# Moving four steps of a hand-ordered attention: modulation, its weights' loads, x2's product, a transposition of maxima

## The chip, the cores and the metric

The kernel runs on one core of a Trainium2 chip. The metric is device time in microseconds (us) of one launch. The kernel before takes 2960.37 us, the median of three runs (2959.13 to 2960.70). One more run was profiled; every duration below comes from it.

## The reference, cut to what matters

A batch of 8 sequences (256 channels x 512 steps) goes through four residual layers. The change touches the first two only.

```
x  = x + L0(x, cond, Wq, Wo)          # masked attention, 8 heads, q = k = v, over 512 positions
x  = x + L1(x, cond, W_emb, ...)      # below, 16 heads, over 256 positions
x  = x + L2(...)                      # oscillator, 512 steps in sequence
x  = x + L3(...)                      # GRU, 512 steps in sequence

# L1
scale, shift = split(cond @ W_emb + b_emb)
xn  = rms_norm(x, g_norm) * (1 + scale) + shift          # the modulation
q, k, v = heads(xn @ W_qkv);  q, k = rms_norm(q, g_q), rms_norm(k, g_k)
o   = softmax(q k' / sqrt(32)) v
out = o + o @ W_out                                      # added to x: "x2"
```

## The kernel before, in words

There are two parts, one after the other: `attention` (L0 and L1) and `scans` (L2 and L3). The change lies in `attention`; `scans` needs all of x2.

`attention` is a list of slots, g = -5 to 79. In each slot a fixed order of calls, written out by hand at the end of the function, gives each engine its instructions; every engine runs its own in that order. The work of the 8 sequences overlaps: `at(g, rel, n)` gives the sequence b and the step r of it that falls in slot g, 8 slots (U) to a sequence.

L0, for each sequence b and each half e of the heads, has four chunks of keys:
- `project` (slots 8b-5 and 8b-4; TensorE line 176, VectorE line 179, ScalarE line 182) makes q; `project_out` transposes it a slot later.
- `scores0` (TensorE line 198, four products of 512 columns a slot; ScalarE line 203 copies them to SBUF).
- `maxima0` (VectorE line 208) takes each row's maximum over a chunk, one chunk a slot.
- `rows0` runs after the fourth chunk, in each slot g = 3 mod 4 from -1 to 59: four 128x128 transpositions (TensorE line 216, one for each chunk's maxima), a copy (ScalarE line 218), then on SyncE's queue a write of the row to DRAM (`row`, line 221) and its load back to all partitions (`bc`, line 222, 1 MB). `bc` has one buffer.
- `weights0` (VectorE line 226 subtracts `bc`, ScalarE line 227 takes the exponential), `values0` (TensorE line 238), `weigh0` (VectorE lines 255 and 256), `masked_out` (line 265).

L1, for each sequence, runs some 11 slots later:
- `normalize` and `modulate` (lines 277 to 296) use `shift` and `G`, made once by `modulation`.
- `modulation` (lines 123 to 148) has two small transpositions, 32 fp32 products of `wemb` with the 8 conditions (line 135; each product is two instructions on TensorE, so the trace counts 64), seven short VectorE steps that end in `shift`, and the addition of the identity to `wout_sb` (line 148). It is called in slot 4.
- `qkv` (TensorE line 305, ScalarE lines 318 and 320), `qkv_norm` (VectorE line 326, GpSimd lines 328 to 330), and a slot later `qkv_out` (TensorE line 340, ScalarE line 344) make v, k and q, one sixth a slot; for the last two sequences two sixths a slot.
- `maxima1` (TensorE line 352, VectorE line 360), `rows1` (line 365), `weights1` (TensorE lines 375 and 384, ScalarE line 390) and `values1` (TensorE line 154, VectorE lines 164 and 165) run for four chunks c of heads, in slots HEADS to HEADS+5. HEADS is 19, 27, 35, 43, 51, 59, 65 and 71.
- `modulated_out` makes x2 (TensorE line 405, VectorE line 410) in two halves, in slots OUT: (25, 27), (33, 35), (41, 43), (49, 51), (57, 59), (65, 67), (71, 72), (77, 78). `modulated_turn` transposes it one slot later.

All of these but `values0` take their PSUM results from one pool of six banks (`bank`), handed out in the order of the calls; a new product waits until the one that had the bank six calls ago has been read.

The weights `wqkv_sb` (3 MB, first read in slot 13) and `wout_sb` (1 MB, first read by line 148, then in slot 25) are loaded on SyncE's queue before the first slot, after `wemb`, the second sequence's x and `wo_sb`. Every DMA of the kernel is issued there.

Of the kernel before, what the change touches and what calls it, by code (L numbers as in the profile page):

```python
# [8 lines left out]
F32 = mybir.dt.float32  # L9
# [5 lines left out]
P = 128  # L15
B, T, D = 8, 256, 512
NJ = D // P
# [7 lines left out]
def attention(ctx, tc, cst, x, cond, wqT, woT, w_emb, b_emb, g_norm, w_qkv, g_q, g_k, w_out, follow):  # L25
# [21 lines left out]
    U = 8  # L47
# [31 lines left out]
    with tc.manual_schedule():  # L79
        nc.sync.dma_start(wq_sb, wqT.rearrange("(k p) e -> p k e", p=P))  # L80
        load(0)
        cst["rest"]()
        vec = wp.tile([12, P], F32, name="vec")
        nc.sync.dma_start(vec[0:8, :], b_emb.rearrange("(f p) -> f p", p=P))
        nc.sync.dma_start(vec[8:12, :], g_norm.rearrange("(f p) -> f p", p=P))
        gq_sb = wp.tile([P, 1], F32, name="gq_sb")
        gk_sb = wp.tile([P, 1], F32, name="gk_sb")
        for i in range(4):
            nc.sync.dma_start(gq_sb[32 * i : 32 * i + 32, :], g_q.unsqueeze(1))
            nc.sync.dma_start(gk_sb[32 * i : 32 * i + 32, :], g_k.unsqueeze(1))  # L90

        wemb = [
            two.tile([P, 2 * D], F32, tag=tag, name=f"wemb_{k}", bufs=bufs)
            for k, (tag, bufs) in enumerate((("qT", 1), ("kT", 1), ("vt", 2), ("vt", 2)))
        ]
        for k in range(NJ):
            nc.sync.dma_start(wemb[k], w_emb[k * P : (k + 1) * P, :])
        load(1)
        wo_sb = fone.tile([P, 2, 256], F32, name="wo_sb")
        nc.sync.dma_start(wo_sb, woT.rearrange("(k p) e -> p k e", p=P))  # L100
        wqkv_sb = wp.tile([P, NJ, 3 * D], F32, name="wqkv_sb")
        nc.sync.dma_start(wqkv_sb, w_qkv.rearrange("(k p) f -> p k f", p=P))
        wout_sb = wp.tile([P, NJ, D], F32, name="wout_sb")
        nc.sync.dma_start(wout_sb, w_out.rearrange("(k p) f -> p k f", p=P))

    gqs = wp.tile([P, 1], F32, name="gqs")
    mhalf = wp.tile([P, 16], F32, name="mhalf")
# [15 lines left out]
    def modulation():  # L123

        nc.vector.tensor_scalar_mul(gqs, gq_sb, SC)
        pv = bank([P, 28], "pvs")
        nc.tensor.transpose(pv, cst["vecs"], ident[0:28, 0:28])
        nc.vector.tensor_copy(cst["vecS"], pv)
        pv = bank([P, 12], "pv")
        nc.tensor.transpose(pv, vec, ident[0:12, 0:12])  # L130
        nc.vector.tensor_copy(vecT, pv)
        pe = bank([P, 8, B], "pe")
        for f in range(8):
            for k in range(NJ):
                nc.tensor.matmul(
                    pe[:, f, :],
                    lhsT=wemb[k][:, f * P : (f + 1) * P],
                    rhs=condT[:, k, :],
                    start=(k == 0),
                    stop=(k == NJ - 1),  # L140
                )
        nc.vector.tensor_tensor(ssT, pe, vecT[:, 0:8].unsqueeze(2).to_broadcast([P, 8, B]), ALU.add)
        nc.vector.tensor_scalar_add(G, ssT[:, 0:NJ, :], 1.0)
        nc.vector.tensor_tensor(G, G, vecT[:, 8:12].unsqueeze(2).to_broadcast([P, NJ, B]), ALU.mult)
        nc.vector.tensor_copy(shift, ssT[:, NJ:8, :])

        for c in range(NJ):
            nc.vector.tensor_add(wout_sb[:, c, c * P : (c + 1) * P], wout_sb[:, c, c * P : (c + 1) * P], ident)
# [57 lines left out]
    def maxima0(b, e, qc):  # L206

        nc.vector.tensor_reduce(  # L208
            mxp0[e].rearrange("p q (h i) -> p q h i", i=32)[:, qc, :, 0], scs[b, e, qc], AX.X, ALU.max
        )  # L210

    def rows0(b, e):

        pt = bank([P, NJ, P], f"pm0_{b}_{e}")
        for qc in range(NJ):
            nc.tensor.transpose(pt[:, qc, :], mxp0[e][:, qc, :], ident)
        mrow = ftwo.tile([P, D], F32, tag="mrow", name=f"mrow0_{b}_{e}", bufs=1)
        nc.scalar.copy(mrow, pt.rearrange("p q n -> p (q n)"))
        bc = bcs[b, e] = ftwo.tile([P, 4, D], F32, tag="bc", name=f"bc_{b}_{e}", bufs=1)
        row = dram.tile([4, D], F32, tag="row", name=f"row_{b}_{e}", bufs=2)  # L220
        nc.sync.dma_start(row, mrow.rearrange("(h i) n -> h i n", i=32)[:, 0, :])
        nc.sync.dma_start(bc, row.rearrange("h n -> (h n)").partition_broadcast(P).rearrange("p (h n) -> p h n", h=4))
# [114 lines left out]
    def qkv_out(b, part, m, qr):  # L337
        pt = bank([P, NJ, P], f"ptqk_{b}_{m}_{part}")
        for c in range(NJ):
            nc.tensor.transpose(pt[:, c, :], qr[:, c * P : (c + 1) * P], ident)  # L340
        ts, tag, g = ((qTs, "qT", gqs), (kTs, "kT", gk_sb))[part]
        if m == 0:
            ts[b] = two.tile([P, NJ, 256], F32, tag=tag, name=f"{tag}_{b}", bufs=1)
        nc.scalar.activation(ts[b][:, :, m * P : (m + 1) * P], pt, AF.Copy, scale=g)
# [56 lines left out]
    def modulated_out(b, m):  # L401
        n = f"{b}_{m}"
        ps = bank([P, D], f"psx2_{n}")
        for c in range(NJ):
            nc.tensor.matmul(  # L405
                ps, lhsT=oTs[b][:, c, m * P : (m + 1) * P], rhs=wout_sb[:, c, :], start=(c == 0), stop=(c == NJ - 1)
            )
        x2 = line(f"x2_{n}")

        nc.vector.tensor_tensor(  # L410
            x2.rearrange("p (m j i) -> p j m i", j=NJ, m=NJ),
            ps.rearrange("p (j m i) -> p j m i", j=NJ, m=NJ),
            xs[b][:, m, :].rearrange("p (j m i) -> p j m i", j=NJ, m=NJ),
            ALU.add,
        )
        return x2
# [41 lines left out]
    def leave(kind):  # L458
        for key in [k for k in left if k[0] == kind]:
            yield *key[1:], left.pop(key)  # L460

    with tc.manual_schedule():
        for g in range(-5, OUT[-1][1] + 2):

            if a := at(g, -4, U):
                scores0(a[0], a[1] // 4, a[1] % 4)
            if a := at(g, 2, U):
                values0(a[0], a[1] // 4, a[1] % 4)
            for a in leave("qt"):
                project_out(*a)  # L470
            if g == OUT[-1][1] + 1:
                cst["soon"]()
            for a in leave("x2"):
                modulated_turn(*a)
            if g - 1 in norms:
                modulate(norms.index(g - 1))
            if a := at(g, 1, U):
                weights0(a[0], a[1] // 4, a[1] % 4)
            if (a := at(g, 2, U)) and a[1] % 4 == 3:
                weigh0(a[0], a[1] // 4)  # L480

            if a := at(g, -5, 2):
                left["qt", a[0], a[1]] = project(*a)
            if a := at(g, U + 2):
                masked_out(a[0])
            if g == 4:
                modulation()
            if g in norms:
                normalize(norms.index(g))
            made = [(part, qkv(*part)) for part in parts.get(g, ())]  # L490
            for a in leave("qkv"):
                qkv_out(*a)
            for b in range(B):
                if g in OUT[b]:
                    m = OUT[b].index(g)
                    left["x2", b, m] = modulated_out(b, m)

            for part, lines in made:
                if lines:
                    qkv_norm(*part, *lines)  # L500
                    left["qkv", *part] = lines[1]
            if a := heads(g, 1):
                rows1(*a)
            a, a1 = at(g, -4, U), heads(g, 0)
            last = a and a[1] % 4 == 3
            if last:
                maxima0(a[0], a[1] // 4, 3)
            if a1:
                maxima1(*a1)
            if a2 := heads(g, 2):  # L510
                values1(*a2)
            if a2 := heads(g, 1):
                weights1(*a2)
            if a and not last:
                maxima0(a[0], a[1] // 4, a[1] % 4)
            if last:
                rows0(a[0], a[1] // 4)
            if (a2 := at(g, -7)) and a2[0] > 1:
                load(a2[0])
            if g == U * B + 2:  # L520
                first.close()
                follow()
                for (b, m), d in x2d.items():
                    nc.sync.dma_start(
                        cst["x2T"][:, :, b, m * P : (m + 1) * P], d.rearrange("p (j n) -> p j n", j=NJ)
                    )
# [486 lines left out]
```

## Time and profile before

| | us |
|---|---|
| median of three runs (lowest, highest) | 2960.37 (2959.13, 2960.70) |
| the profiled run: its own time | 2958.41 |
| the profiled run: span, first to last instruction | 2956.6 |
| attention, up to the scan's first product | 881.3 |
| TensorE busy, whole span | 2720.4 |
| VectorE busy | 2124.6 |
| ScalarE busy | 1720.9 |
| GpSimd busy | 1049.1 |

The profile gives, for each engine, busy time by line and by stretch of time, the waits with what released them, and the instructions in order of time. In an "in order of time" view a row is the start, the time from the first start to the last end of a run of equal instructions, the engine, line and operation, out<-in, shape and count; in brackets stands the idle time before it and the engine or DMA that ended it. PE is TensorE, DVE VectorE, ACT ScalarE, POOL GpSimd, SP SyncE. PEclk is the clock granted to TensorE, 1.00 being full speed.

### The profile page before, as it was taken

How to read it: one execution, taken by the hardware profiler on the slowest of the kernel's cores; microseconds unless marked ns; L12 is line 12 of the kernel's file. 1: busy time of each engine (PE TensorE's matmuls, PEld its weight loads, DVE VectorE, ACT ScalarE, POOL GpSimd, SP SyncE). 2: the span in 40 equal slices, each digit the busy share in tenths (PEclk: the TensorE clock that was granted, in tenths of full speed). 3: DMA queues.
4: the chain of work that ended last, by engine and by line, in shares of the span. 5: the costliest groups of instructions: out<-in, count | busy, mean ns of one | idle time of the engine just before them, and what ended most of it. 6: DMA issues, size and time to landing. Idle time of an engine off the chain costs nothing.

```text
span 2956.6 us, 159809 instructions
## 1 busy us (share of the span) xinstructions
PE 2720.4 (92%) x67258; PEld 1930.5 (65%) x67258; DVE 2124.6 (72%) x8948; ACT 1720.9 (58%) x8427; POOL 1049.1 (35%) x2945
## 2 busy tenths in 40 slices
PE   6789999999988999999999999999999999999997
PEld 3234444444546777777777777777777777777776
DVE  4866676666446777777777777777777777777773
ACT  4655566554335666666666666666666666666551
POOL 0233123312313444444444444444444444444442
PEclk7989999999999999999999999999999999999998
DMA  3110101000600000000000000000000000000000
GB/s 143 40 40 29 40 26 47 29 33 23 129 15 4 7 6 7 6 7 7 7 6 7 6 7 7 6 6 7 7 7 7 6 7 7 6 7 6 6 7 6
DMA packets 27559, 57.60 MB, mean 19 GB/s; under 512 B 2816, under 2 KB 17164, under 8 KB 24788
## 3 DMA queue, kind: packets, MB, share of 16 engines
q1 hardware_dynamic: 26836, 47.36, 5.3%
q8 instruction: 526, 8.62, 1.2%
q14 instruction: 197, 1.61, 0.2%
HBM read 40.15 MB, written 7.21 MB: 16 GB/s over the span
## 4 chain that ended last, share of the span: by engine, by line
PE 39%; DVE 24%; ACT 5%; issue 3%; ACTq 0%; POOL 0%; DVEq 0%; POOLq 0%
PE pg L744 19%; PE ic L709 18%; DVE icT L901 5%; DVE qn L902 5%; ACT tT L609 4%; DVE hqs L862 3%; DVE own L759 3%; DVE sqmm L858 2%; DVE v L761 2%; DVE hz L789 2%; DVE own L778 1%; ACT sqmm L847 1%; DVE own L784 1%; PE psx L405 1%; ACTq L609 0%
## 5 line engine op out<-in xcount | busy, mean ns | idle before, releaser
L709 PE MATMUL ic<-cT_sb,tT 128*8 128x128 f32 x32736 | 1086.1, 273 | 82.3 <-ACT tT L609 45.6
L709 PEld LDWEIGHTS ic<-cT_sb,tT 128*8 128x8 f32 x32736 | 760.1, 89 | 339.8 <-ACT tT L609 268.5
L744 PE MATMUL pg<-whh_sb,hz 128*32 128x128 f32 x24576 | 820.9, 275 | 49.4 <-DVE hz L789 17.6
L609 ACT ACTIVATE tT<-qn 128x16 f32<-128x16 f32 x2046 | 440.8, 216 | 636.9 <-DVE qn L902 516.4
L744 PEld LDWEIGHTS pg<-whh_sb,hz 128*32 128x32 f32 x24576 | 669.5, 110 | 123.1 <-DVE hz L789 122.9
L901 DVE STREAM_TRANSPOSE icT<-ic 128x64 f32<-128x64 f32 x2048 | 504.2, 246 | 67.6 <-PE ic L709 63.2
L902 DVE SCALAR_TENSOR_TENSOR qn<-icT,hqs 128x16 f32<-128x16 f32 x2048 | 350.7, 171 | 70.1
L704 POOL TENSOR_TENSOR W<-W,cx 128x128 f32<-128x128 f32 x765 | 297.3, 389 | 256.6 <-ACT cx L690 256.4
L697 POOL TENSOR_TENSOR W<-cx,us 128x128 f32<-128x128 f32 x255 | 116.9, 458 | 445.0 <-ACT cx L690 445.0
L858 DVE SCALAR_TENSOR_TENSOR sqmm<-sqmm,qn 128x32 f32<-128x32 f32 x768 | 153.5, 200 | 151.4 <-ACT sqmm L847 122.4
L862 DVE TENSOR_TENSOR hqs<-W,sqmm 128x32 f32<-128x32 f32 x1020 | 199.9, 196 | 46.1 <-DVE own L784 1.0
L723 PE MATMUL gi<-wih_sb,x3T 128*32 128x384 f32 (+2 forms) x3072 | 201.5, 379 | 0.5 <-POOL x3T L914 0.5
L690 ACT ACTIVATE cx<-qn 128x32 f32<-128x32 f32 x1280 | 200.9, 213 | 0.0
L227 ACT ACTIVATE sc<-sc,negT 128x2048 f32<-128x2048 f32 x64 | 128.6, 2010 | 89.2 <-DVE sc L226 79.2
L305 PE MATMUL psqkv<-wqkv_sb,xnT 128*128 128x512 f32 x384 | 174.8, 600 | 0.2 <-DVE oT L165 0.2
L690 ACT ACTIVATE cx<-p 128x32 f32<-128x32 f32 x1020 | 149.8, 217 | 32.4 <-DVE p L857 1.6
L226 DVE TENSOR_TENSOR sc<-sc,bc 128x2048 f32<-128x2048 f32 x64 | 147.8, 2310 | 11.9 <-DMA bc<-row 11.9
L203 ACT COPY sc<-s 128x512 f32<-128x512 f32 x256 | 132.1, 617 | 40.6 <-PE s L198 40.4
L759 DVE STREAM_TRANSPOSE own<-pg 128x128 f32<-128x128 f32 x256 | 84.8, 331 | 94.8 <-PE pg L744 94.8
L208 DVE TENSOR_REDUCE mxp<-sc 128x4 f32<-128x2048 f32 x64 | 145.8, 2279 | 6.7 <-ACT sc L203 6.7
L690 ACT ACTIVATE cx<-q 128x32 f32<-128x32 f32 x1020 | 145.5, 213 | 0.0
L847 ACT ACTIVATE sqmm<-qn 128x32 f32<-128x32 f32 x768 | 140.5, 183 | 0.6
(149 smaller groups left out, 3364.0 us busy)
## 6 DMA issues: line engine op xcount, KB each, us to landing
bc<-row SPq DMA_DIRECT2D x16, 1024.0 KB
x<-in_x SPq DMA_DIRECT2D x8, 512.0 KB
out<-o SPq DMA_DIRECT2D x256, 16.0 KB
wqkv_sb<-in_L_cond_W_qkv SPq DMA_DIRECT2D x1, 3072.0 KB
wih_sb<-in_L_cond_W_ih SPq DMA_DIRECT2D x4, 768.0 KB
whh_sb<-in_L_cond_W_hh SPq DMA_DIRECT2D x4, 768.0 KB
x2d<-x2o SPq DMA_DIRECT2D x11, 256.0 KB
x2T<-x2d SPq DMA_DIRECT2D x11, 256.0 KB
```

What stands on the lines that cost most here:

```text
L305: nc.tensor.matmul(ps, lhsT=xnTs[b][:, c, m * P : (m + 1) * P], rhs=wqkv_sb[:, c, part * D : (part + 1) * D], start=(c == 0), stop=(c == N ...
L609: nc.scalar.activation(tT, src[:, half * HM : (half + 1) * HM, :], AF.Tanh)
L690: nc.scalar.activation(c[:, i], x, AF.Copy, scale=f)
L704: nc.gpsimd.tensor_tensor(W[:, i + 1 : 5], W[:, i + 1 : 5], c, ALU.add)
L709: nc.tensor.matmul(ps[32 * j : 32 * j + B, :], lhsT=tT[k // HM][:, k % HM, :], rhs=cT_sb[:, k, j * P : (j + 1) * P], start=(k == 0), stop= ...
L723: nc.tensor.matmul(gi_ps[rows(j), g0:g1, :], lhsT=x3T[c][:, k, :], rhs=wih_sb[:, k, g0:g1, j * P : (j + 1) * P], start=(k == 0), stop=(k = ...
L744: nc.tensor.matmul(pg_ps[rows(j), :], lhsT=hzs[tau % 3][:, k, 32 * g : 32 * g + 32], rhs=whh_sb[:, k, g, j * P : (j + 1) * P], start=((k, ...
L759: nc.vector.transpose(pgt.rearrange("p m n -> p (m n)"), pg_ps)
L858: stt(mm, sq, LIN[s], qs, ALU.subtract, ALU.mult)
L862: nc.vector.tensor_sub(hq, W[:, s], mm)
L901: nc.vector.transpose(icT.rearrange("p m n -> p (m n)"), ic[:, half * 64 : half * 64 + 64])
L902: stt(qn[:, m2, :], icT[:, :, 0:B], IC[s], hq[:, m2, :], ALU.mult, ALU.add)
```

## The change

- `modulation` is called in slot 1, not 4; its last step, the identity added to `wout_sb` (four VectorE instructions), becomes `add_identity` and is called in slot 8, just ahead of `normalize`.
- The loads of `wqkv_sb` and `wout_sb` become `load_weights`, called at the end of slot -1, behind that slot's `rows0`.
- In each slot, `modulated_out` stands ahead of `qkv_out`. Both run in slots 25, 27, 33, 35, 41, 43, 49, 51, 57, 59, 65 and 71. Only TensorE's order changes by it: `qkv_out` has no VectorE step, and `modulated_out` no ScalarE step.
- `rows0` follows the fourth `maxima0` at once, ahead of `maxima1`, `values1` and `weights1` of the slot. These run beside it in slots 19, 27, 35, 43, 51, 59 (`maxima1`) and 23, 31, 39, 47, 55 (`values1`, `weights1`); in the other slots of `rows0` nothing stands between.

No instruction is added or removed. The diff:

```diff
@@ -98,10 +98,14 @@
-        wqkv_sb = wp.tile([P, NJ, 3 * D], F32, name="wqkv_sb")
+    wqkv_sb = wp.tile([P, NJ, 3 * D], F32, name="wqkv_sb")
+    wout_sb = wp.tile([P, NJ, D], F32, name="wout_sb")
+
+    def load_weights():
+
         nc.sync.dma_start(wqkv_sb, w_qkv.rearrange("(k p) f -> p k f", p=P))
-        wout_sb = wp.tile([P, NJ, D], F32, name="wout_sb")
         nc.sync.dma_start(wout_sb, w_out.rearrange("(k p) f -> p k f", p=P))
@@ -143,6 +147,8 @@
         nc.vector.tensor_copy(shift, ssT[:, NJ:8, :])
+
+    def add_identity():
 
         for c in range(NJ):
             nc.vector.tensor_add(wout_sb[:, c, c * P : (c + 1) * P], wout_sb[:, c, c * P : (c + 1) * P], ident)
@@ -483,17 +489,19 @@
-            if g == 4:
+            if g == 1:
                 modulation()
+            if g == U:
+                add_identity()
             if g in norms:
                 normalize(norms.index(g))
             made = [(part, qkv(*part)) for part in parts.get(g, ())]
-            for a in leave("qkv"):
-                qkv_out(*a)
             for b in range(B):
                 if g in OUT[b]:
                     m = OUT[b].index(g)
                     left["x2", b, m] = modulated_out(b, m)
+            for a in leave("qkv"):
+                qkv_out(*a)
@@ -505,6 +513,7 @@
             if last:
                 maxima0(a[0], a[1] // 4, 3)
+                rows0(a[0], a[1] // 4)
             if a1:
                 maxima1(*a1)
             if a2 := heads(g, 2):
@@ -513,10 +522,10 @@
             if a and not last:
                 maxima0(a[0], a[1] // 4, a[1] % 4)
-            if last:
-                rows0(a[0], a[1] // 4)
             if (a2 := at(g, -7)) and a2[0] > 1:
                 load(a2[0])
+            if g == -1:
+                load_weights()
```

## The prediction, as put on record

> **What bounds the kernel now.** First the busy times by stretch: the first 148 us, the rest of attention, the scans. Columns: us of PE, PEld, DVE, ACT, POOL, then the granted clock, DMA share, GB/s.
>
> ```profile
> 0.00:148.00 148.00, 104.51 (x550) 44.19 (x554) 97.37 (x74) 81.85 (x127) 18.40 (x23) 0.84 0.25 91
> 148.00:881.00 733.00, 680.79 (x4716) 318.87 (x4708) 458.87 (x425) 382.28 (x629) 193.60 (x159) 0.95 0.15 42
> 881.00:2956.60 2075.60, 1935.06 (x62000) 1567.41 (x62000) 1568.38 (x8451) 1256.81 (x7673) 837.13 (x2763) 1.00 0.03 7
> ```
>
> The scans (2075.6 us) hold no changed line and wait for the last x2, so they start earlier or later by what attention gains. From 148 to 881 TensorE is busy 93%: there a wait on TensorE is lost unless a later wait shrinks by it. The first 148 us have 43 us of idle TensorE and no engine that is full; waits decide. So I read the start in order of time, TensorE first:
>
> ```profile
> 23.91 7.27 PE L198 MATMUL s<-qm 32*128 32x512 f32 x24
> 42.16 1.94 PE L238 MATMUL pc<-sc,qtok 128*32 128x512 f32 x8 [10.98 <-ACT sc L227]
> ...
> 59.37 10.60 PE L135 MATMUL pe<-condT,wemb 128*128 128x8 f32 x64
> ```
>
> TensorE stands idle for 10.98 us, then spends 10.60 us in modulation. VectorE beside it:
>
> ```profile
> 39.93 2.28 DVE L208 TENSOR_REDUCE mxp<-sc 128x4 f32<-128x2048 f32 x1
> ...
> 70.00 0.22 DVE L142 TENSOR_TENSOR ssT<-pe,vecT 128x64 f32<-128x64 f32 x1 [9.83 <-PE pe L135]
> ...
> 71.48 2.28 DVE L208 TENSOR_REDUCE mxp<-sc 128x4 f32<-128x2048 f32 x1
> ```
>
> Modulation halts VectorE for 9.83 us; from 71.48 on VectorE runs without a gap to 93.8, so it sets the pace there. The 10.98 us come from the first `bc`: its row is issued at 24.63 (behind 4 MB of weights), `bc` only at 32.99, 7.7 us of it a wait for the row; VectorE's subtraction starts at 37.72.
>
> Then the slots where `rows0` meets L1's work. Slot 31, TensorE, then VectorE:
>
> ```profile
> 348.23 0.38 PE L365 MATMUL pm<-ident,mxp 128*128 128x128 f32 x2
> 348.54 1.07 PE L154 MATMUL pc<-ex,vt 128*32 128x256 f32 x16
> ...
> 352.35 0.66 PE L216 MATMUL pm<-ident,mxp 128*128 128x128 f32 x4
> 354.21 1.14 PE L198 MATMUL s<-qm 32*128 32x512 f32 x8 [1.21 <-DVE oT L165]
> ```
>
> ```profile
> 349.66 2.28 DVE L208 TENSOR_REDUCE mxp<-sc 128x4 f32<-128x2048 f32 x1
> ...
> 353.64 0.42 DVE L165 TENSOR_TENSOR oT<-pc,r 128x256 f32<-128x256 f32 x1
> ```
>
> The maxima that line 216 needs are done at 351.9; `values1` and `weights1` fill TensorE until 352.35, so line 216 waits for nothing. Last, slot 59, where q's transposition does wait:
>
> ```profile
> 687.62 1.11 PE L340 MATMUL ptqk<-ident,qr 128*128 128x128 f32 x4 [3.40 <-POOL qr L330]
> 688.53 4.82 PE L405 MATMUL psx<-wout_sb,oT 128*128 128x512 f32 x8
> ...
> 696.64 1.07 PE L238 MATMUL pc<-sc,qtok 128*32 128x512 f32 x8
> ```
>
> x2's product, whose inputs are ready, queues behind that wait. After 148 us the waits of line 340 on GpSimd sum to 15.6 us (8 of them).
>
> [...] at 156.21 line 216 waits 3.27 us with the next slot's ready scores behind it. [...] the stretch 424 to 429 has a mean clock of 0.66 and 452 to 456, right after slot 39's wait, one of 0.57, each the mean of 3.4 us at 0.50 and the rest at 1.00. [...] the 8 KB row took 7.7 us behind the weights, 1.8 us (54.63 to 56.39) with an empty queue.
>
> **The change, part by part.**
>
> *Modulation and weights (slots -1 to 8).* The loads now stand behind `bc`: row at 24.63, landed 26.4, `bc` issued then, and 4.7 us (32.99 to 37.7) later, at 31.1, it is there instead of at 37.7. The weights follow, 4 MB at some 400 GB/s (the rate at 25 to 30 us), done near 40; first read in slots 8 (93.8 us) and 13 (135.57), so 50 us of cover. `wemb` lies in the first 4 MB of the queue, landed near 21 (rates summed from the stretches of 5 us).
> TensorE: scores of slots 0 and 1 are two thirds of the 7.27 us, to 28.8. Then modulation. Its products run at half clock there (0.50 from 22 to 46 us): from 65 to 70 us, at 0.50, 28 took 5.0 us, 0.179 each, so 64 take 11.4, to 40.6 with the two transpositions. VectorE's steps to `shift` (70.00 to 70.84) end at 41.5, and slot 1's maxima start there, not at 39.93: 1.6 us late. Slot 2's scores come at 40.6 to 43.0, `values0` 0.9 later than 42.16; with half clock lasting a little longer I carry 2.6 us late to slot 4. There the queue finds no modulation: its maxima begin after line 179 at 59.25 + 2.6 + 0.7 = 62.5 instead of 71.48. Gain 8.9. `bc`'s 6.6 us are not added: modulation's own end (40.6) would hide a `bc` of 37.7. Bounds: 6 (half clock goes on to slot 5) and 10.6 (nothing late). The identity's 0.89 us goes to slot 8, where VectorE idles 1.42 (scores' copies) and 1.92 (`bc`) around it: nothing; 0.9 if that cover went.
>
> *x2 first, slots 25 to 57 with half 0.* The transposition did not wait there; order alone. kT's copy comes 3.5 us later and is read two slots on. Nothing; bounds 0 and +0.5 each (ScalarE behind it).
>
> *x2 first and `rows0` early, slots 27, 35, 43, 51.* By slot 27: x2's product starts at 290.45 instead of 292.43, ends 294.0; the transposition (qr ready at 291.9) ends 294.5. x2's addition (0.7) and the maxima (2.28) on VectorE end at 297.0, not 299.0. Line 216 ends 297.4. `maxima1`'s second half still waits for qT, whose copy ScalarE runs at 297.17 to 297.84 behind `normalize`, which is not changed: ends 298.6. Before, line 216 came after that, and the next scores ended at 301.33, held by banks that VectorE frees (2.06 us instead of 1.14). Now VectorE frees them 0.8 earlier and one bank belongs to the already copied maxima: end near 299.8. Gain 1.5 each, 6.0. Bounds 0.7 (bank waits stay) and 2.7 (both waits, 1.49 and 1.21).
> *Slot 19*, no x2: line 216 (1.05) falls into the 4.65 us wait for qT. With the bank, 1.6.
> *Slot 59:* x2's product from 684.2, maxima done 690.8 (from 687.8 + 0.7 + 2.3), `maxima1` ends behind qT's copy (692.9) at 693.6; `values0` there instead of 696.64. Gain 3.0.
> *Slot 65:* the wait of 1.73 goes, but qT's copy, hidden by x2's product until now, shows some 0.6. Gain 1.2. *Slot 71:* the 3.44 goes, 0.8 of copy shows, and a little queueing: 3.1 (bounds 1.5 and 4.8, the latter with x2's product at full clock: 3.6 for 5.29).
>
> *`rows0` early, slots 23, 31, 39, 47, 55.* By slot 31: line 216 now stands behind `rows1` (348.5) and its fourth transposition needs the maxima of 351.9: done 352.25, after about 3.0 us idle. Behind it in TensorE's queue stand `values1` (1.9, to 354.15) and `weights1` (1.95, to 356.1). The next scores wait for banks: the second for `values1`'s result, 1.75 + 0.42 on VectorE after 354.15, so 356.4; the third and fourth for the first exponentials of line 390 (356.8, 357.3). They end at 357.6, before at 355.28: 2.35 lost, five times 11.8. `bc` gains nothing: its one buffer is freed by the next slot's subtraction as before. Bounds: 0.5 each if the maxima come early enough, 5.8 if two half-clock windows follow each wait (each 3.4 us long, 1.7 lost).
>
> *Clock.* One more half-clock window in slot 31's kind, where four of five had one already (+1.7), against the one in slot 71 that should go (-1.7): 0; bounds -5 and +9.
>
> *Sum:* 8.9 + 6.0 + 1.6 + 3.0 + 1.2 + 3.1 = 23.8 gained, 11.8 lost: 12.0 less. The profiled run took 2958.4 (span 2956.6 and 1.8 around it), so 2946.4; the median of the runs is 2.0 above that run: 2948.4.
>
> **Rivals.**
> 1. *The moved transposition makes it slower.* Line 216's wait in slots 23 to 55 sends TensorE to half clock through `values1`, `weights1` and the next slot. For: the wait is near 3 us[...]; after the 3.27 us wait at 156.21 the clock was halved. Against: after 2.80 us at 121.88 it was not. Three windows each: 2.35 + 3 x 1.7 = 7.45, times 5 = 37.3; 13.5 more than the 23.8 gained, so 2973.9. It decides from 23.8 / 5 = 4.8 us a slot.
> 2. *The wait of slots 23 to 55 costs next to nothing*, since the 1.21 us bank wait goes and others shrink: 0.4 each. 2960.4 - 21.8 = 2938.6. For: that wait does end later than the stall; against: VectorE's queue has the maxima behind line 326 in both.
> 3. *The start gains little:* TensorE's modulation at half clock delays every later step of slots 2 to 5, and `bc`'s chain takes over: 2.5 instead of 8.9. 2954.8. For: three engines are near each other there. Against: VectorE's 9.83 us halt is gone in any case.
>
> **Chances and numbers.** Forecast 0.54, rival 1 0.16, rival 2 0.16, rival 3 0.14. Predicted 2948.4. The forecast's own range is 2940 to 2956 (start +-3, slots 23 to 55 +-5, clock). The range runs from 2936 (half of rival 2 below its centre) to 2964, which leaves out most of rival 1. About 0.2% (5.9 us, below 2954.5 or above 2966.3) is what a measurement can tell from no change. Faster: 0.48 of the forecast, all 0.16 of rival 2, 0.06 of rival 3: 0.70. Slower: 0.12 of rival 1. The rest, 0.18, within.
>
> **What would show it.** Start: line 135 at about 29 us, no 9.8 us halt of VectorE near 60, slot 4's maxima near 62.5. Slot 31: line 216 with an idle of about 3 us released by line 208, ahead of line 154. Line 340's waits on GpSimd: only slot 19's 1.1 us left. The period between slots 35 and 43, 98.97 us now, becomes 99.8. The scan's first product at 869 instead of 881.3. I am wrong if slot 31's kind loses over 4.8 us, or if slot 4's maxima start after 68.

## The result, and the profile after

The change makes the kernel slower: 2982.21 us, the median of five runs (2971.95 to 2989.34), against 2959.91 of five runs of before (2957.82 to 2960.70). The ratio is 1.0072 with a 95% interval of 1.0046 to 1.0098. The forecast was 2948.4, the range 2936 to 2964. Two statements ahead of the prediction are wrong: the scans go through 256 steps, not 512 (no number of the prediction rests on it), and in the program as built one instruction does go: ScalarE has 175 semaphore waits ahead of the scans, where before has 176.

The profiled run of the change took 2974.9 us (span 2973.1, 16.5 more than before's), so it is one of the better of its five. All that follows accounts for those 16.5 us. The line numbers of the new kernel are shifted: 208, 216, 305, 340, 344 and 405 are now 214, 222, 311, 346, 350 and 411, and in the scans 609, 709, 902 are 618, 718, 911.

Busy times by stretch again, up to 148 us, to the scan's first product, and the scans:

```profile
0.00:148.00 148.00, 114.46 (x562) 49.24 (x563) 98.74 (x74) 85.28 (x130) 18.71 (x23) 0.85 0.25 91
148.00:894.00 746.00, 693.06 (x4697) 329.98 (x4695) 457.78 (x423) 379.07 (x624) 193.81 (x159) 0.93 0.14 41
894.00:2973.10 2079.10, 1937.71 (x62000) 1565.25 (x62000) 1570.79 (x8453) 1254.54 (x7674) 840.87 (x2763) 1.00 0.03 7
```

The middle has grown by 13 us, at a mean clock of 0.93 for 0.95: TensorE is busier with the same products. The scans, untouched, have grown by 3.2 us from their first product (881.28 in before, 894.54 now) to the end; between the round times of the view it is 3.5.

The start did what it should. VectorE, in order of time:

```profile
33.78 2.29 DVE L232 TENSOR_TENSOR sc<-sc,bc 128x2048 f32<-128x2048 f32 x1 [0.69 <-DMA bc<-row]
...
45.69 0.23 DVE L146 TENSOR_TENSOR ssT<-pe,vecT 128x64 f32<-128x64 f32 x1 [9.39 <-PE pe L139]
...
66.01 2.28 DVE L214 TENSOR_REDUCE mxp<-sc 128x4 f32<-128x2048 f32 x1
```

`bc` is there at 33.8, modulation's halt of 9.39 us has moved to slot 1, and slot 4's maxima start at 66.01 (before 71.48), though this run was 2.7 us late at slot 0 already: eight products of line 204 took 2.09 us at 10.25, where before's took 1.14. That is the luck of the run and not the change, for the run x2_only below, which is like before up to slot 25, was 2.1 late there too.

The transposition of the maxima waits as predicted. Slot 31 on TensorE:

```profile
343.31 0.38 PE L371 MATMUL pm<-ident,mxp 128*128 128x128 f32 x2
...
347.08 0.33 PE L222 MATMUL pm<-ident,mxp 128*128 128x128 f32 x1 [3.06 <-DVE mxp L214]
347.34 1.07 PE L160 MATMUL pc<-ex,vt 128*32 128x256 f32 x16
...
351.04 2.51 PE L204 MATMUL s<-qm 32*128 32x512 f32 x8
```

And slot 47, the same work after the same wait:

```profile
551.47 0.48 PE L222 MATMUL pm<-ident,mxp 128*128 128x128 f32 x1 [3.06 <-DVE mxp L214]
551.88 1.94 PE L160 MATMUL pc<-ex,vt 128*32 128x256 f32 x16
...
559.03 3.51 PE L204 MATMUL s<-qm 32*128 32x512 f32 x8
562.47 1.94 PE L244 MATMUL pc<-sc,qtok 128*32 128x512 f32 x8
```

The 3.06 us are equal; what follows takes 1.94 us where slot 31 took 1.07. The granted clock of the stretch 549 to 568 is the last column but two:

```profile
549.00:568.00 19.00, 16.53 (x92) 7.50 (x93) 6.80 (x5) 6.75 (x11) 4.18 (x3) 0.55 0.22 84
```

In before the same stretch of work has a mean clock of 0.91:

```profile
547.00:566.00 19.00, 17.80 (x133) 7.27 (x129) 11.09 (x9) 10.20 (x17) 8.23 (x6) 0.91 0.24 84
```

The clock's records show 17.1 us at half, five windows of 3.41, behind slots 47 and 55; 10.2 behind slots 43 and 51; 3.4 behind 23 and 39; nothing behind 27, 31 and 35.

TensorE's waits after 148 us: line 346's for GpSimd, 15.6 us before, have shrunk to 1.1 (slot 19's). In their place (us in total, how often, the longest):

```profile
PE pm L222 <- DVE mxp L214: 30.9, 12, 3.3
```

Where the 16.5 us come from is read from VectorE's maxima, one a slot: start of the slot's maxima, before, and how much later (+) or earlier (-) in the other kernels' profiled runs.

| slot | before | the change | no_rows | rows_only | filler | hoist |
|---|---|---|---|---|---|---|
| 0 | 28.11 | +2.7 | +2.1 | +0.4 | +2.7 | +0.4 |
| 4 | 71.48 | -5.5 | -6.1 | +1.8 | -5.5 | -6.2 |
| 18 | 186.19 | -4.2 | -7.4 | +1.6 | -6.2 | -9.9 |
| 20 | 213.30 | -4.4 | -7.9 | +0.5 | -7.3 | -9.7 |
| 24 | 266.57 | -1.5 | -9.5 | +9.0 | -5.9 | -8.7 |
| 32 | 365.34 | -1.8 | -8.0 | +13.2 | -2.3 | -9.7 |
| 40 | 464.32 | +1.3 | -8.4 | +16.9 | +3.0 | -8.4 |
| 48 | 563.28 | +11.7 | -9.0 | +26.3 | +5.1 | -9.6 |
| 56 | 662.25 | +22.0 | -7.8 | +30.3 | +4.7 | -10.2 |
| scan | 881.28 | +13.3 | -14.4 | +34.8 | -4.0 | -18.9 |

### The profile page after: what moved, and what is told of

It reads as the page before. It is cut to its first block, busy times and chain, and to the rows that moved or that the text cites. A ratio compares the mean times of both kernels' runs of the same rounds, so it can differ in the third digit from the quotient of the medians.

```text
span 2973.1 us, 159804 instructions
## 1 busy us (share of the span) xinstructions
PE 2745.2 (92%) x67258; PEld 1944.5 (65%) x67258; DVE 2127.3 (72%) x8948; ACT 1718.9 (58%) x8427; POOL 1053.4 (35%) x2945
## 4 chain that ended last, share of the span: by engine, by line
PE 59%; DVE 28%; ACT 7%; issue 4%; DMA 1%; POOL 0%; ACTq 0%; SPq 0%; DVEq 0%; POOLq 0%
PE pg L753 19%; PE ic L718 18%; PE psqkv L311 5%; DVE icT L910 5%; DVE qn L911 5%; ACT tT L618 4%; PE pc L244 4%; DVE hqs L871 3%; PE s L204 3%; DVE own L768 3%; DVE sqmm L867 2%; DVE v L770 2%; PE pc L160 2%; DVE mxp L214 2%; DVE hz L798 2%
```

## The experiments

Each stands beside runs of before on the same chip, whose medians were 2958.91, 2958.97 and 2958.76 in the three groups. The first group takes the change apart.

**no_rows: all but the moved transposition.**
```diff
-                rows0(a[0], a[1] // 4)      # behind maxima0
...
+            if last:
+                rows0(a[0], a[1] // 4)      # at the slot's end
```


> The change without its fourth edit: the transposition of the maxima stays at the slot's end. Theory A (the moved transposition makes TensorE wait some 3 us in slots 23, 31, 39, 47, 55, and the clock drops to half after it for several windows): nothing left of the loss; the start gains 8, slot 59 2.4, slot 65 1.2, slot 71 3.1, so about 15 less than before, near 2945, with a spread of runs as narrow as before's 3 us, and about two half-clock windows a period. Theory B (any shift of the work against the clock's windows, as by the start, sets off the long half-clock stretches): still above 2965, with runs spread over 10 us.

Measured 2947.92 (2944.64 to 2952.73, 19 runs), ratio 0.9972 [0.9961, 0.9984]. It is as theory A has it, though the gain is 11 us, not 15, and the spread 8 us, not 3. No half-clock stretch over 6.8 us after slot 20. The fourth edit alone turns a gain of 11 us into a loss of 22.

**rows_only: the moved transposition alone,** the reverse of that diff, in before.


> Before, with the fourth edit alone: the transposition of the maxima right behind the last maximum. Theory A: five waits of 3 us of line 216, 3.1 us lost in each of those slots at full clock and 2 to 8 us more where the clock halves, so 15 to 40 us more than before, 2975 to 3000, and runs spread over 10 us. Theory B: the waits alone, five times 3.1 less some 8 us won in slots 19 to 59, about 2968, and no half-clock stretch above 7 us.

Measured 2992.93 (2991.76 to 2996.47, 5 runs), ratio 1.0122 [1.0104, 1.0140]: 34 us more, with stretches of 17.1 us at half clock behind slots 23 and 47. Theory B's 2968, the waits alone, is out. Only the spread (4.7 us) was narrower than theory A had it.

**start_only: modulation, identity and loads alone.**
```diff
+            if g == 1:
                 modulation()
+            if g == U:
+                add_identity()
...
+            if g == -1:
+                load_weights()
```


> Before, with modulation in slot 1, the identity in slot 8 and the weights' loads behind the first bc. Theory A: 8 us less than before, near 2952, runs close together. Theory B: the start's shift sets off the half-clock stretches after 300 us, 2965 or more. A third reading, that the start gives nothing since its gain is taken back before slot 19, would give 2960.

Measured 2955.74 (2953.07 to 2958.89, 14 runs), ratio 0.9993 [0.9980, 1.0006]: the medians differ by 3 us, not 8, and the interval does not tell that from nothing. Theory B is out, there is no loss; the profiled run was 8.0 ahead at the scan's first product and 4.9 at its end. The rest went into the scans (start_act below).

**x2_only: x2's product first, alone.**
```diff
-            for a in leave("qkv"):
-                qkv_out(*a)
             for b in range(B):
                 if g in OUT[b]:
...
+            for a in leave("qkv"):
+                qkv_out(*a)
```


> Before, with x2's product ahead of the transpositions of q and k alone. Theory A: nothing in slots 27 to 51, where qT's copy behind normalize ends the slot either way, and 2.4 + 1.2 + 3.1 = 6.7 in slots 59, 65 and 71: near 2953. Theory B: any shift sets off half-clock stretches, 2965 or more.

Measured 2947.37 (2946.53 to 2951.24, 11 runs), ratio 0.9968 [0.9953, 0.9983]. In its trace slots 27 to 51 give next to nothing, as expected (1.1 us between slots 26 and 58), and slot 59 and later 9.2, for 6.7 expected. This part alone is worth what no_rows is worth in all: with the start's edits no_rows is 2.9 us further ahead at the scan's first product, and its scans take 2.4 back.

The second group asks what of the moved transposition costs.

**filler: the change, with TensorE kept at work through the wait** in slots 23, 31, 39, 47 and 55, ahead of the fourth transposition.
```diff
+            if qc == NJ - 1:
+                for _ in range(fill):       # 13 in those slots, else 0
+                    nc.tensor.matmul(pt[:, qc, :], lhsT=ident, rhs=ident, start=True, stop=True)
             nc.tensor.transpose(pt[:, qc, :], mxp0[e][:, qc, :], ident)
```


> The change, and in slots 23, 31, 39, 47, 55 thirteen spare products of the identity with itself ahead of the fourth transposition, written where that transposition then writes: TensorE works on through its 3 us wait for the maxima, and no step that matters is moved. Theory A (the clock halves because of the wait): each of those slots loses the 3.1 us of the wait's detour as slot 31 of the change did, not the 8.5 of slots 47 and 55; some 15 to 20 us less than the change on the same chip, near or a little below before's time, half-clock stretches of 10 to 17 us gone behind those slots. Theory B (the 8.5 us are the banks' and VectorE's queue): no faster than the change, some 2975 to 2985.

Measured 2959.45 (2954.38 to 2965.18, 22 runs), ratio 1.0009 [0.9997, 1.0021]: 23 us less than the change, by adding work. Slot 47:

```profile
548.74 3.07 PE L224 MATMUL pm<-ident 128*128 128x128 f32 x26
551.96 0.33 PE L225 MATMUL pm<-ident,mxp 128*128 128x128 f32 x1 [0.15 <-DVE mxp L214]
552.22 1.07 PE L160 MATMUL pc<-ex,vt 128*32 128x256 f32 x16
```

The clock around it, with no half-clock stretch behind any of the five slots:

```profile
548.00:567.00 19.00, 18.85 (x173) 10.86 (x171) 8.66 (x7) 9.50 (x16) 5.73 (x5) 1.00 0.22 85
```

`values1` stands as late behind the maxima as in the change, but runs in 1.07 us, not 1.94. From one slot to the next the five slots now cost 1.5, 3.1, 1.5, 1.5 and 1.5 us (change: 2.9, 3.1, 3.1, 8.5, 8.5): the detour of 3.1, less the half-clock window worth 1.65 that before had in four of them. This is the split of the cost: 3.1 for the order, the rest for the clock.

**hoist: the change, with the fourth chunk's maxima earlier on VectorE,** where it idles.
```diff
+            a = at(g, -4, U)
+            last = a and a[1] % 4 == 3
+            if last:
+                maxima0(a[0], a[1] // 4, 3)
             made = [(part, qkv(*part)) for part in parts.get(g, ())]
...
             if last:
-                maxima0(a[0], a[1] // 4, 3)
                 rows0(a[0], a[1] // 4)
```


> The change, with the fourth chunk's maxima ahead of the slot's q, k, v part on VectorE: in slot 31 VectorE idles there for 3.3 us, so the maxima are ready before TensorE reaches the moved transposition. Theory A: no wait of line 216's kind in slots 23 to 55, and in slots 27 to 59 none either; the detour and the half clock behind it go, 20 to 25 less than before: 2934 to 2940. Theory B (an early transposition costs by the order of the banks): 2950 or more though the wait is gone.

Measured 2939.71 (2937.78 to 2944.78, 12 runs), ratio 0.9950 [0.9929, 0.9971]. Slot 31, VectorE and then TensorE:

```profile
336.18 2.28 DVE L214 TENSOR_REDUCE mxp<-sc 128x4 f32<-128x2048 f32 x1
```
```profile
338.71 0.38 PE L371 MATMUL pm<-ident,mxp 128*128 128x128 f32 x2
338.93 0.60 PE L222 MATMUL pm<-ident,mxp 128*128 128x128 f32 x4
339.46 1.07 PE L160 MATMUL pc<-ex,vt 128*32 128x256 f32 x16
```

The maxima are done at 338.5, all four transpositions run in one go, no wait. The early place itself is harmless; theory B is out.

**hoist_late: early maxima as in hoist, `rows0` back at the slot's end.**


> The same early maxima, with the transposition at the slot's end, where before has it. Tells whether the early maxima or the early transposition is worth something once the wait is gone. If the transposition's early place is good for nothing there: as the kernel with early maxima and early transposition within 3 us. If it helps in slots 19 to 59 by filling the wait for qT: some 5 to 8 us slower than that one, near 2945.

Measured 2943.57 (2940.54 to 2948.59, 19 runs), ratio 0.9957 [0.9944, 0.9969]; 3.9 slower than hoist on that chip, between the two readings. Each against before on its own chip, hoist gains 8.3 us more than no_rows; 4.4 of them come with the early maxima and 3.9 with the early place.

**rows_chosen: early only beside `maxima1`.**
```diff
+                if not heads(g, 2):
+                    rows0(a[0], a[1] // 4)
...
+            if last and heads(g, 2):
+                rows0(a[0], a[1] // 4)
```


> The change with the transposition early only where maxima1 stands beside it (slots 19 to 59) and at the end in slots 23 to 55. Theory A: the long half-clock stretches of slots 23 to 55 go, as in the kernel without the fourth edit, and 1 to 2 us are won in each of slots 19 to 59: 2938 to 2946. Theory C (the 2.3 us waits in slots 43 and 51 halve the clock on their own, 5.6 us each): no better than without the fourth edit, 2948 or more.

Measured 2945.23 (2940.94 to 2953.10, 22 runs), ratio 0.9957 [0.9946, 0.9968]: inside theory A's span, but only 2.7 below no_rows, which ran on another chip. Theory C holds in part: in its trace the waits of 2.3 us in slots 27 and 51 are each followed by 6.8 us at half clock, those in slots 35 and 43 are not.

The third group takes the start apart.

**start_act: start_only, with one ScalarE instruction more before the scans.**
```diff
         nc.scalar.activation(tanh, condS.rearrange("p (s m) b -> p s m b", s=2), AF.Tanh)
+        nc.scalar.activation(tanh, condS.rearrange("p (s m) b -> p s m b", s=2), AF.Tanh)
```


> The kernel with the start's edits alone, and one ScalarE instruction more just ahead of the scans (tanh of the conditions, made twice over). The kernel with the start's edits alone ran 8 us ahead at the scan's first product and then lost 3.1 of it over the scan, in single steps that are 0.2 to 0.3 us long. Theory D (ScalarE's instructions before the scan are one fewer, 175 semaphore waits for 176[...]): one more puts it back, the scan's 255 steps take 2014.0 us for 2017.1, the whole some 3 less than the start's edits alone, near 2952.5. Theory E (the scan's 3 us come from elsewhere, as the loads or buffers): 2955.7, the scan at 2017.

Measured 2952.23 (2935.04 to 2958.00, 14 runs), ratio 0.9980 [0.9964, 0.9996]. 255 steps of the scan took 2013.5 us; in start_only 2017.1, in before 2014.0. Theory D's 2014 holds, and theory E's 2017 is out.

**hoist_act: the same instruction in hoist.**


> The change with the maxima early on VectorE, and the same ScalarE instruction more ahead of the scans. Theory D: some 3 less than without it, 2936 to 2937, the scan at 2014. Theory E: 2939.7.

Measured 2936.60 (2934.60 to 2940.40, 8 runs), ratio 0.9937 [0.9915, 0.9958], the scan 2013.1 for 2017.3. The fastest version found, ahead of both kernels.

**mod_only and weights_only: the start's halves.**
```diff
-    def load_weights():      # mod_only: the loads stay where before has them
...
-            if g == 1:           # weights_only: modulation() and add_identity() in slot 4
```


> Before, with modulation in slot 1 and the identity in slot 8; the weights' loads stay ahead of the first bc. By the prediction modulation's end at 40.6 hides a bc of 37.7, so this alone gives what the start's edits give together, within 1 us: slot 4's maxima 6 to 9 us earlier than before. If the loads matter: half of it or less.

> Before, with the weights' loads behind the first bc, modulation in slot 4 as before. bc at 31 to 34 instead of 37.7 lets slot 1 start some 4 to 6 us earlier and nothing takes it back: slot 4's maxima 4 to 6 earlier, as much as modulation's move alone gives, so that the two are one gain and not two; near 2954. If modulation's halt in slot 4 takes it back: as before.

mod_only 2950.78 (2947.56 to 2957.82, 22 runs), ratio 0.9989 [0.9973, 1.0004]; weights_only 2956.90 (2935.86 to 2960.80, 22 runs), ratio 0.9997 [0.9977, 1.0017]. Neither is told from before by its interval, since ten of the 53 runs of before on that chip took 2934 to 2940; the traces are clearer. From slot 0 to slot 4 mod_only gains 8.1, weights_only 6.6, both together 8.2 in the change and 6.6 in start_only: one gain, not two. The scan takes 2013.4 in mod_only and 2016.7 in weights_only. So the move of the loads buys nothing beside modulation's and costs the scans 3 us.

## Why the prediction was wrong

*Start.* Predicted 8.9, measured 8.2 between slots 0 and 4 (6.6 in start_only). Right in size, and the two halves' overlap and the free identity in slot 8 too. One reading under it was wrong: from 65 to 70 us before has 24 of line 135's 64 instructions, not 28, 0.214 us from one to the next and not 0.179; the moved 64 took 13.8 us for the 11.4 worked out, and slot 1 lost 3.7 us, not 1.6. That nothing else would follow from the loads' move was wrong too: +3.2 in the scans.

*x2 first, and slots 27 to 51.* Predicted 6.0, measured about nothing: the four stretches around slots 27, 35, 43 and 51 changed by -3.4, 0, +1.9 and +1.8. At full clock the gain was 0.3 a slot (slots 26 to 28 and 34 to 36): the next scores still wait for banks (slot 35's took 2.66 us, 2.06 in before). The -3.4 is for the most part luck: before has 6.8 us at half clock behind slot 27, this run has none. And where two waits of 1.49 and 1.21 us had stood apart, one of 2.3 stands now, which in slots 43 and 51 halved the clock (3.8 us each against slot 35, 1.7 of it given back).

*Slot 19.* Predicted 1.6, measured 0.2. *Slots 59, 65, 71.* Predicted 7.3, measured 8.8.

*Slots 23, 31, 39, 47, 55: the step that failed.* The prediction had "They end at 357.6, before at 355.28: 2.35 lost, five times 11.8", and for the clock "0; bounds -5 and +9". The mechanism was right to the wait's length (3.0 us forecast, 3.06 measured), and so was the queue behind it. The term was mis-sized: 26.1 us in the profiled run. Of that, by the second group, the order costs 3.1 a slot (0.8 more than worked out: the next scores took 2.51 us, 1.14 in before, beside ScalarE's 2.07 us of reading the banks, line 396), and the rest is half clock. Rival 1 named this and its threshold, 4.8 us a slot; the mean came to 5.2. That its 2973.9 lies near the profiled run is luck, since it had 7.45 a slot. It got 0.16, and the range cut most of it off, because I counted half-clock windows by what before had there (one in four of five slots) and added one for all five together. What before showed was a wait of 1.2 us; the new one, of 3.06, is nearly as long as one half-clock window (3.41). And the 3.4 us at 0.50 in each of the two stretches that the prediction read (424 to 429 and 452 to 456) are how long the half clock lasted; how long a wait has to be was not shown by them: slot 39's was 1.2 us.

*Sum.* Late at slot 0 +2.7; start -8.2; slots 4 to 18 +1.3; slot 19 -0.2; the five slots +26.1; slots 27 to 51 +0.3; slot 59 to the scan -8.8; scans +3.2: +16.4 of 16.5 us. Against the 2946.4 forecast for the profiled run it is 28.5 us too long. The failed step makes 14.3 of them (26.1 for 11.8), slots 27 to 51 make 6.3, the scans 3.2, the late slot 0 2.7; the other terms come to about 2. The median of the change lies 7 us above its profiled run; those runs have no trace.

**Why 3.06 us cost 3 or 8.5.** In the clock's records of before and of the change every stretch from one change of the clock to the next, at half (3.41, 6.83, 10.24, 17.07 or 23.89 us) and at full, is a whole number of 3.41 us. So all changes of a run lie on one grid; its steps are the windows spoken of here. Counted from the span's first instruction, an edge lies at 1.49 us in before and at 0.97 in the change. Laid over the waits for the maxima in slots 23 to 55 of the change and of rows_only (18 waits, 2.27 to 3.06 us), it parts them: in 13 a single window holds 2.03 us or more of the wait, and at its end the clock halves each time; in 5 the wait falls across an edge and no window holds more than 1.89, and it never does. Slot 31: 1.70 and 1.36. Slot 47: 2.11 and 0.95. The wait of 2.80 us at 121.88, which the prediction held against rival 1, fell across an edge too (1.89 and 0.92); the one of 3.27 us at 156.21 had 2.15 in one window.

The line is less sharp in other traces. Of the same wait in slots 27 to 59 of filler and rows_chosen (ten, 2.27 to 2.29 us) four with 2.18 us or more in one window halved the clock, three with 1.48 to 1.73 did not, but three with 1.76 to 1.87 did. Over all 14 traces, from 148 to 870 us, each of the 68 full-clock windows in which TensorE stood idle for 2.0 us or more was followed by half clock, and so were 22 of the 40 with 1.5 to 2.0. So the price depends on the phase of the program against the windows. No run moves the phase alone, so this rests on the traces; the spread of the runs decides nothing, since it was 17 us for the change's five and 3 for before's five, but 26 to 31 for the larger groups of before. In the change a wait of 2.27 us was enough (slot 43). Waits of 1.20 us in before were followed by half clock too, in slots 23, 39, 47 and 55, where `weights1`'s products stand beside them (those of 1.21 us in slots 27, 35, 43 and 51 were not), so 2 us is no lower limit. Not settled: why some stretches last five windows and others one with the same products behind them.

**Why the scans slowed.** The ten kernels with the loads moved have 175 semaphore waits of ScalarE before the scans, the others 176. In start_only 23 of the scan's 2046 tanh on ScalarE (line 619) start 0.28 us later behind their input `qn` than the rest; in before, mod_only and start_act 9 do (two more, near the loop's start, are late in every kernel). One of the 23, on VectorE and on ScalarE:

```profile
1122.99 0.17 DVE L912 SCALAR_TENSOR_TENSOR qn<-icT,hqs 128x16 f32<-128x16 f32 x1
```
```profile
1123.55 0.33 ACT L619 ACTIVATE tT<-qn 128x16 f32<-128x16 f32 x2 [1.04 <-DVE qn L912]
```

`qn` is there at 1123.16; ScalarE takes it up at 1123.55, and no wait in the trace holds it. The trace shows where these late starts lie: with ScalarE's instructions counted from its first one, semaphore waits included, each is the 64th of a group of 128, and no tanh in that place starts on time. It is so in all 14 traces: 23 late ones where ScalarE has one instruction fewer (255 steps in 2016.4 to 2017.3 us), 9 in the six others, start_act and hoist_act among them (2013.1 to 2014.0). One instruction fewer ahead of the scans moves that place onto 14 more tanh; one more takes the 3 us away again. So the count of ScalarE's instructions is the cause. What ScalarE does in these 0.28 us no trace shows.

## What to carry to other kernels

Before an instruction is moved ahead in TensorE's queue, look for when its inputs are made, and move their maker first: the same early transposition cost 34 us (rows_only) or gained 4 (hoist against hoist_late), depending on one VectorE step that had an idle gap waiting for it. Price a new TensorE wait not by its length but by what runs behind it at half clock, as soon as 2.0 us of it can fall in one window of 3.41 us (in the 14 traces half clock followed on all 68 full-clock windows with that much idle time), and expect that price to vary with where the wait falls: 3.06 us cost 3.1 in slot 31 and 8.5 in slot 47. When a part that was not touched changes its time, compare the instruction counts ahead of it: one ScalarE instruction was worth 3.6 us here (start_only against start_act).

## What the runs showed of the hardware that was not expected

- Waits of 2.27 us were enough to halve TensorE's clock, for 10.2 us (slots 43 and 51), and waits of 3.06 us for 17.1 (slots 47 and 55); 13 spare products (26 instructions, 3.07 us) in each of five waits made the kernel 23 us faster.
- One ScalarE instruction more or fewer ahead of a 2014 us loop changed it by 3.6 us (start_only 2017.1, start_act 2013.5) and 4.2 us (hoist 2017.3, hoist_act 2013.1), through 14 delays of 0.28 us, each at the 64th of 128 ScalarE instructions.
- Before's own runs reached from 2933.6 to 2964.4 us (53 runs): in the ten below 2941 the mean granted clock was 0.982 to 0.984, in the others 0.973 to 0.977. So a single run of it says little about 0.3%.
